# An element-wise causal attention kernel: one fold moved to another step, two sums joined, and the work at the start put in another order

## The chip, the cores and the metric

The kernel runs on one core of one Trainium2 chip. Its engines work side by side and meet only at semaphores: TensorE multiplies matrices (PE in the profile, PEld for its weight loads), VectorE (DVE) and GpSimd (POOL) do element-wise work and reductions, ScalarE (ACT) does exponentials, activations and copies out of the matrix accumulators, SyncE (SP) issues transfers. GpSimd issues transfers too, among them all that add into their target. The metric is the device time of one execution in microseconds (us). The kernel before takes 4008.09 us (median of three runs, 4007.45 to 4010.71).

## The reference

Input x has 8 batches of 512 tokens with 256 features. Four blocks follow each other, each added to x after a layer norm: attention A, a feed-forward net, attention B, and the same feed-forward net again.

```python
x = x + attn_a(layernorm(x), Wq, bq, Wk, bk, Wv, bv, Wo, bo)
x = x + ffn(layernorm(x), w1, w2, h1, h2, w3)
x = x + attn_b(layernorm(x), W_attn, b_attn, W_proj, b_proj)
x = x + ffn(layernorm(x), w1, w2, h1, h2, w3)
```

The change lies in attention A. It attends not between tokens but inside each token and head: with 16 heads of 64 channels,

```python
scores = einsum('bshq,bshk->bshqk', Q / 8, K)     # 64 x 64 for each token and head
scores = where(triu(ones((64, 64)), 1), -inf, scores)
w = softmax(scores, axis=-1)
attn = einsum('bshqk,bshk->bshq', w, V)
```

A score is the product of two single numbers, so no matrix engine can help: for every token and head there are 2080 products, exponentials and weighted values. They are done element by element, with the tokens on the 128 partitions.

## The kernel before

**Groups.** Attention A takes the work in groups of 128 tokens by 4 heads (256 columns). There are 8 batches, 4 column groups g and 4 token tiles i, so 128 groups. For each group TensorE projects queries and values (`qv`) and keys (`pk`), ScalarE copies keys and queries to SBUF (`keep_qk`, L761, L762).

**Units.** The lower triangle of each 64 by 64 score matrix is cut into squares on the diagonal's steps: one square of side 32 for each head, two of 16, then 8, 4, 2, 1. A group has four units, and these are its four steps: unit 0 is the squares of 32 of two heads, unit 1 all squares of 16, unit 2 the squares of 32 of the other two heads, unit 3 all small ones. For each unit:

- `scores` multiplies queries and keys (L784), on GpSimd for units 0 and 2, in two instructions, and on VectorE for units 1 and 3;
- `exps` takes the exponential on ScalarE (L798);
- `weigh` multiplies by the values on VectorE (L808), so that a tile holds exponentials and weighted values side by side;
- units 0 to 2 are then **halved**: `halve` (L814) has GpSimd issue a transfer that adds the second half of the 4096-column tile onto the first, 1 MB;
- units 0 and 2 are halved once more by an addition on GpSimd, `fold` (L819);
- `gather` (L845) sums what is left along the rows, on VectorE, into a tile `red`;
- `add_rows` (L852) adds `red` into the group's accumulator `acc` on GpSimd. `small_squares` (L835 and L852) does this for the squares of 2 and 1;
- at the end `invert` (L856) and `divide` (L860) make the quotient, and TensorE transposes and projects it out.

**Steps.** `AttentionA.step(n)` writes out one step by hand. All engines but SyncE keep the order in which these lines run. There are 512 units, and a step has work of several of them: the scores of unit n, the exponentials of n-1, the weighing and halving of n-2, folds and gathers of n-3 and n-4, the division of n-5. A step has three parts, each ended by a `yield`. In what follows the steps of a group are named by n mod 4, which is the unit whose scores are computed.

| step | part | GpSimd, before | VectorE, before |
|---|---|---|---|
| 0 | A | scores of unit 0, first half; halving of unit 2; second half | weighing of unit 2; reciprocal |
| 0 | B | division; **fold of unit 0** | |
| 1 | A | | weighing of unit 3; gather of unit 1 |
| 1 | B | sum of unit 1; small squares; fold of unit 2 | scores of unit 1 |
| 1 | C | | **gather of unit 0** |
| 2 | A | scores of unit 2, first half; halving of unit 0; second half | weighing of unit 0 |
| 2 | B | **sum of unit 0** | |
| 2 | C | | gathers of unit 2 and of the squares of 8 and 4 |
| 3 | A | halving of unit 1 | weighing of unit 1 |
| 3 | B | sums of unit 2, of the squares of 8 and of 4 | scores of unit 3 |

The unit numbers belong to the group that the unit is of: in steps 0 and 1 the weighing, folding and gathering is of the group that began four steps before. A list `self.sums` holds sums until part B of the next step, or of the same one where the gather stood in part A.

**Between the parts** the main loop (at the end of `fast_path`) puts other work. `done` is a generator of the feed-forward nets and attention B of batches whose attention A is complete. It starts at step 75, and from there on is advanced in proportion to the steps, so that it fills the gaps of attention A. Before that, two things happen once. `fit_qkv(g)` subtracts a row from the projection weights of column group g (on GpSimd, but for g = 0 on VectorE), has SyncE load a bias row into them and store them to a scratch tensor in DRAM, out of which `load_w` loads them later. `prep = later_weights()` is a generator that prepares the later weights and bounds the scores: small work on braw (L421 to L432), products for w3 (L451), subtractions (L456) on GpSimd, loads and stores on SyncE, squares on ScalarE (L373, L374), 96 matrix products with one column (L382). It has 30 pieces.

`measure(b)` computes the layer norm's scales of batch b on VectorE and GpSimd.

Of the kernel before, what the change touches and what calls it, by code (L numbers as in the profile page):

```python
# [9 lines left out]
F32 = mybir.dt.float32  # L10
# [3 lines left out]
ALU = mybir.AluOpType  # L14
AX = mybir.AxisListType

P = 128
# [9 lines left out]
GW = GH * C  # L27
NG = HID // GW
# [256 lines left out]
def fast_path(ctx: ExitStack, tc: tile.TileContext, k, t, flag):  # L285

    nc = tc.nc
# [8 lines left out]
    ap_ = ctx.enter_context(tc.tile_pool(name="ap", bufs=2))  # L296
# [42 lines left out]
    def fit_qkv(g):  # L339

        wqv, wk = fitted[g]
        eng = nc.vector if g == 0 else nc.gpsimd
        qv_last = last_qv[:, g * 2 * GW : (g + 1) * 2 * GW].unsqueeze(1).to_broadcast([P, DC, 2 * GW])
        eng.tensor_tensor(wqv, wqv, qv_last, ALU.subtract)
        k_last = last_k[:, g * GW : (g + 1) * GW].unsqueeze(1).to_broadcast([P, DC, GW])
        eng.tensor_tensor(wk, wk, k_last, ALU.subtract)
        nc.sync.dma_start(wqv[P - 1 : P, DC - 1, :], t.b_qv[g : g + 1, :])
        nc.sync.dma_start(wk[P - 1 : P, DC - 1, :], t.b_a[1:2, g * GW : (g + 1) * GW])
        nc.sync.dma_start(wqv_d[g].rearrange("p (c f) -> p c f", c=DC), wqv)
        nc.sync.dma_start(wk_d[g].rearrange("p (c f) -> p c f", c=DC), wk)  # L350
# [253 lines left out]
    class AttentionA:  # L604
# [33 lines left out]
        def step(self, n):  # L638
# [13 lines left out]
            b, i, g, u = self.at(n + 40)  # L652
            if u == 0 and g == 0 and i == 0 and b > 0:
                self.x[b] = load_x(b)
            b, i, g, u = self.at(n + 10)
            if u == 0 and g == 0 and i == 0:
                self.measure(b)
            b, i, g, u = self.at(n + 8)
            if u == 0 and g == 0:
                self.live["xn"] = normed(self.x[b][:, i, :], *self.rn[b, i], "a")  # L660
            b, i, g, u = self.at(n - 5)
            if u == NU - 1:
                self.invert(b, i, g)
            b, i, g, u = self.at(n - 4)
            if u == 1:
                self.gather(b, i, g, u)
            b, i, g, u = self.at(n + 7)
# [11 lines left out]
            b, i, g, u = self.at(n - 5)  # L679
# [3 lines left out]
            if u == NU - 1:  # L683
                self.small_squares(b, i, g)

            b, i, g, u = self.at(n - 4)
            if u == 0:
                self.fold(b, i, g, u)
            b, i, g, u = self.at(n - 3)
            if u == 2:  # L690
                self.fold(b, i, g, u)
# [14 lines left out]
                self.project(b, i, g)  # L706
            yield
            b, i, g, u = self.at(n - 4)
            if u == 2:
                self.gather(b, i, g, u)  # L710
            b, i, g, u = self.at(n - 5)
            if u == 0:
                self.gather(b, i, g, u)
            b, i, g, u = self.at(n - 3)
            if u == NU - 1:
                self.gather(b, i, g, u)
            b, i, g, u = self.at(n - 7)
            if u == NU - 1:
                nc.scalar.copy(self.live["att"], self.live.pop("pta"))
# [118 lines left out]
        def gather(self, b, i, g, n_u):  # L838


            w = self.live.pop((b, i, g, n_u))
            for n, off, nsq, cols in squares(units[n_u]):
                if n > 2:
                    red = ap_.tile([P, 2, nsq * n], F32, tag=f"red{nsq * n}", name=f"red_{b}_{i}_{g}_{n_u}_{n}", bufs=2 + (n < 32))
                    nc.vector.tensor_reduce(red, self.columns_of(w, n, off, nsq), AX.X, ALU.add)  # L845
                    self.sums.append((b, i, g, n, cols, red))

        def add_rows(self, b, i, g, n, cols, part):

# [491 lines left out]
    with tc.manual_schedule(engines={ET.PE, ET.DVE, ET.Activation, ET.Pool}):  # L1341
        a = AttentionA()
        prep = later_weights()
        fit_qkv(0)
        weights = None
        done, spent = after_a(), 0
        for n in range(-10, a.steps):
            for part, _ in enumerate(a.step(n)):
                if n >= 2:
                    next(prep, None)  # L1350
                while 3 * spent * each < total * (3 * (n - each - 11) + part + 1):
                    spent += next(done)
            if 0 <= n < NG - 1:
                fit_qkv(n + 1)
        for _ in done:
            pass
    judge()
# [86 lines left out]
```

## Time and profile before

| what | value |
|---|---|
| median of three runs | 4008.09 us |
| the profiled execution, its own time | 4009.55 us |
| its span in the profile | 4007.6 us |
| VectorE busy | 3376.7 us (84%) |
| GpSimd busy | 3098.1 us (77%) |
| TensorE busy | 2958.0 us (74%) |
| ScalarE busy | 2337.2 us (58%) |
| transfers of GpSimd's queue, share of the 16 DMA engines' span | 62.9% |
| additions of `red` into `acc` on GpSimd, 128x256, 384 of them | 759 ns each |
| the same, 128x128, 256 of them | 701 ns each |
| folds (L819), 256 of them | 2512 ns each |

The profile is one execution as the hardware profiler recorded it. Busy time is the time in which an engine had an instruction at work, its share is of the span. The profile also lists groups of instructions with the mean time of one and the idle time of the engine just before them, the waits by engine with what ended them, and the instructions in order of time. A line number is that of the kernel's text, and a tile has its program name with the buffer number left out. Records of GpSimd overlap a little, so the distance from one start to the next is the better measure of what an instruction takes there.

### The profile page before, as it was taken

The page shows a single profiled execution, that of the slowest core. Times are in us where ns is not written, and L with a number is a line of the kernel's source. Part 1 is how long each engine was busy: PE and PEld are TensorE (multiplying, and loading weights), DVE is VectorE, ACT ScalarE, POOL GpSimd, SP SyncE. Part 2 cuts the span into 40 slices and gives each one's busy share as a digit, 9 for nine tenths or more (in the row PEclk, how much of TensorE's full clock was granted, in tenths as well). Part 3 has the DMA queues.
Part 4 walks back from the last instruction along what each step waited for, and adds up shares of the span by engine and source line. Part 5 has one row for each costly group of instructions (what it writes and reads, how often), then busy time and mean ns, then how long its engine had stood idle before and what let it go on. Part 6 is the DMA issues. An engine that isn't in the chain of part 4 may idle for free.

```text
span 4007.6 us, 37678 instructions
## 1 busy us (share of the span) xinstructions
PE 2958.0 (74%) x12328; PEld 2012.2 (50%) x12328; DVE 3376.7 (84%) x3777; ACT 2337.2 (58%) x3145; POOL 3098.1 (77%) x3051
## 2 busy tenths in 40 slices
PE   1543478777876888768787788768787778768988
PEld 0311145355653656346553566346653556436847
DVE  4899988998889888998989988998889988897115
ACT  2433465666755766666755767567656667555342
POOL 6688888887888887887888888888888878886211
PEclk7555689888987989889897889879898899879999
DMA  8566777668776777668776688668877687767304
GB/s 240 114 141 145 146 182 182 147 161 199 199 162 126 195 188 196 150 147 210 174 192 139 168 198 214 147 131 198 195 181 151 154 199 205 155 133 210 126 29 167
DMA packets 118653, 671.07 MB, mean 167 GB/s; under 512 B 12704, under 2 KB 31915, under 8 KB 43824
## 3 DMA queue, kind: packets, MB, share of 16 engines
q0 software_dynamic: 78336, 570.46, 62.9%
q1 hardware_dynamic: 40112, 98.11, 6.8%
q8 instruction: 100, 1.64, 0.2%
q14 instruction: 105, 0.86, 0.1%
HBM read 255.90 MB, written 9.96 MB: 66 GB/s over the span
## 4 chain that ended last, share of the span: by engine, by line
DVE 38%; PE 16%; POOL 14%; DMA 12%; issue 8%; ACT 8%; POOLq 0%; DVEq 0%; ACTq 0%
DVE red L845 15%; DMA w<-w 12%; DVE w L808 10%; PE ph L1120 5%; ACT w L798 3%; POOL w L819 3%; DVE ws L808 3%; POOL w L784 3%; PE pqkb L1167 3%; DVE ws L784 3%; POOL acc L852 3%; DVE w L784 2%; POOL w L814 2%; DVE acc L856 2%; POOL h L1036 2%
## 5 line engine op out<-in xcount | busy, mean ns | idle before, releaser
L798 ACT ACTIVATE w<-w 128x2048 f32<-128x2048 f32 x384 | 734.2, 1913 | 653.8 <-POOL w L784 440.8
L1120 PE MATMUL ph<-h,hidden 128*128 128x512 f32 x4096 | 1047.9, 412 | 77.4 <-POOL h L1036 45.5
L784 POOL TENSOR_TENSOR w<-k 128x1024 f32<-128x1024 f32 x512 | 1076.2, 2102 | 9.6 <-ACT k L762 9.0
L1120 PEld LDWEIGHTS ph<-h,hidden 128*128 128x128 f32 x4096 | 795.3, 196 | 282.1 <-POOL h L1036 55.9
L808 DVE TENSOR_TENSOR w<-w,qv 128x1024 f32<-128x1024 f32 x768 | 899.8, 1213 | 22.4 <-ACT w L798 22.3
L845 DVE TENSOR_REDUCE red<-w 128x128 f32<-128x1024 f32 (+1 forms) x384 | 601.8, 1567 | 171.6 <-DMA w<-w 94.6
L819 POOL TENSOR_TENSOR w<-w 128x1024 f32<-128x1024 f32 x256 | 643.1, 2512 | 72.5 <-DMA w<-w 71.9
L814 POOL DMA_DIRECT2D w<-w x384 | 337.1, 878 | 339.7 <-issue 134.8
L852 POOL TENSOR_TENSOR acc<-acc,red 128x256 f32<-128x256 f32 (+1 forms) x640 | 471.0, 736 | 152.3 <-DVE red L845 124.5
L845 DVE TENSOR_REDUCE red<-ws 128x256 f32<-128x2048 f32 (+1 forms) x256 | 435.5, 1743 | 0.0
L746 PE MATMUL qv<-wqv,xnta 128*128 128x512 f32 x512 | 299.3, 715 | 89.9 <-DVE ws L808 82.4
L808 DVE TENSOR_TENSOR ws<-ws,qv 128x1024 f32<-128x1024 f32 (+3 forms) x512 | 294.7, 638 | 49.4 <-ACT ws L798 49.4
L1052 PE MATMUL pw<-xnt,gate 128*128 128x512 f32 (+2 forms) x1152 | 298.8, 419 | 24.9 <-ACT silu L1028 18.0
L784 DVE TENSOR_TENSOR w<-qv,k 128x1024 f32<-128x1024 f32 x256 | 301.3, 1219 | 3.6
L784 DVE TENSOR_TENSOR ws<-qv,k 128x1024 f32<-128x1024 f32 (+3 forms) x512 | 299.8, 648 | 0.0
L868 PE MATMUL bank<-ident,acc 128*128 128x128 f32 x256 | 64.3, 341 | 287.5 <-ACT k L761 287.1
L798 ACT ACTIVATE ws<-ws 128x1920 f32<-128x1920 f32 x128 | 231.5, 1809 | 75.3 <-DVE ws L784 74.7
L1052 PEld LDWEIGHTS pw<-xnt,gate 128*128 128x128 f32 x1152 | 227.6, 213 | 82.1 <-ACT silu L1028 22.3
L1229 ACT ACTIVATE eb<-psb 128x256 f32<-128x256 f32 (+3 forms) x512 | 182.2, 443 | 146.6 <-PE psb L1226 146.3
L1146 PE MATMUL pof<-w,h 128*128 128x256 f32 x1024 | 247.9, 396 | 19.4 <-ACT h L1085 19.4
L1085 ACT ACTIVATE h<-ph,s_sb 128x512 fp32r<-128x512 f32 (+1 forms) x256 | 171.1, 688 | 145.9 <-PE ph L1120 144.6
L856 DVE RECIPROCAL acc<-acc 128x256 f32<-128x256 f32 x128 | 223.2, 1744 | 12.3 <-POOL acc L852 12.3
(143 smaller groups left out, 4723.5 us busy)
## 6 DMA issues: line engine op xcount, KB each, us to landing
w<-w POOLq DMA_DIRECT2D x384, 1024.0 KB, 7.7
hidden<-in_h POOLq DMA_DIRECT2D x128, 1024.0 KB, 7.9
gate<-in_w12p POOLq DMA_DIRECT2D x32, 1024.0 KB, 9.0
w<-w_d SPq DMA_DIRECT2D x16, 1024.0 KB, 12.0
wqv<-wqv_d SPq DMA_DIRECT2D x31, 512.0 KB
wo<-in_wo SPq DMA_DIRECT2D x32, 256.0 KB, 7.4
wbqk<-wbqk_d SPq DMA_DIRECT2D x8, 1024.0 KB
w<-in_h SPq DMA_DIRECT2D x8, 1024.0 KB, 7.0
```

The source lines that it names most:

```text
L746: nc.tensor.matmul(qv.rearrange("p j f -> p (j f)"), xnt[:, c, :], wqv[:, c, :], start=(c == 0), stop=(c == DC - 1),)
L784: eng.tensor_tensor(e, rows(q).to_broadcast(shape), columns(kt[:, 0]).to_broadcast(shape), ALU.mult)
L798: nc.scalar.activation(e, e, AF.Exp, scale=C**-0.5)
L808: nc.vector.tensor_tensor(ev, e, columns(qv[:, 1]).to_broadcast(list(e.shape)), ALU.mult)
L814: nc.gpsimd.dma_start(w[:, :2048], w[:, 2048:], accum_op=ALU.add)
L819: nc.gpsimd.tensor_tensor(w[:, :1024], w[:, :1024], w[:, 1024:2048], ALU.add)
L845: nc.vector.tensor_reduce(red, self.columns_of(w, n, off, nsq), AX.X, ALU.add)
L852: nc.gpsimd.tensor_tensor(rows, rows, part.rearrange("p a (x i) -> p a x i", i=n), ALU.add)
L856: nc.vector.reciprocal(acc[:, 0, :], acc[:, 0, :])
L1052: nc.tensor.matmul(pj[:, toks], w[:, m % 4, j, c, :], xs[:, p, c, toks], start=(p == 0 and c == 0), stop=(p == 1 and c == DC - 1),)
L1120: nc.tensor.matmul(pss[j], w[:, j, c, :], h_in(p, c), start=(p == 0 and c == 0), stop=(p == 1 and c == MC - 1),)
L1146: nc.tensor.matmul(po, h(0, c)[:, i * P : (i + 1) * P], w3[:, c, :], start=(c == 0), stop=False)
```

## The change

Four things are changed.

1. The fold of unit 0 moves from part B of step 0 to part C of the step 3 before it, two parts earlier. The gather of unit 0 moves from part C of step 1 to part C of step 0.
2. The gathers of units 0 and 2 write the two halves of one tile `red`, and one `add_rows` over all 256 columns adds both. The sum of unit 0 in step 2 goes away. The tile of the squares of 32 has one buffer, where it had two.
3. `measure(0)` runs before `fit_qkv(0)`.
4. `fit_qkv(1)`, `(2)`, `(3)` run after steps 4, 14 and 24, where they ran after steps 0, 1 and 2. `prep` is advanced once a step, in part C from step 3 on, where it was advanced in each of the three parts from step 2 on.

```diff
             if u == 0 and g == 0 and i == 0:
-                self.measure(b)
+                if b > 0:
+                    self.measure(b)
...
-            b, i, g, u = self.at(n - 4)
-            if u == 0:
-                self.fold(b, i, g, u)
             b, i, g, u = self.at(n - 3)
             if u == 2:
                 self.fold(b, i, g, u)
...
             b, i, g, u = self.at(n - 4)
-            if u == 2:
-                self.gather(b, i, g, u)
-            b, i, g, u = self.at(n - 5)
-            if u == 0:
+            if u in (0, 2):
                 self.gather(b, i, g, u)
             b, i, g, u = self.at(n - 3)
             if u == NU - 1:
                 self.gather(b, i, g, u)
+            if u == 0:
+                self.fold(b, i, g, u)
...
                 if n > 2:
-                    red = ap_.tile([P, 2, nsq * n], F32, tag=f"red{nsq * n}", name=f"red_{b}_{i}_{g}_{n_u}_{n}", bufs=2 + (n < 32))
-                    nc.vector.tensor_reduce(red, self.columns_of(w, n, off, nsq), AX.X, ALU.add)
-                    self.sums.append((b, i, g, n, cols, red))
+                    if n_u != 2:
+                        self.live["red", n] = ap_.tile(
+                            [P, 2, GW // 2], F32, tag=f"red{n // 32}", name=f"red{n}_{b}_{i}_{g}", bufs=1 if n == 32 else 3
+                        )
+                    red = self.live["red", n]
+                    part = red[:, :, cols.start // 2 : cols.stop // 2]
+                    nc.vector.tensor_reduce(part, self.columns_of(w, n, off, nsq), AX.X, ALU.add)
+                    if n_u != 0:
+                        self.sums.append((b, i, g, n, slice(0, GW), red))
...
         a = AttentionA()
         prep = later_weights()
+        a.measure(0)
         fit_qkv(0)
...
             for part, _ in enumerate(a.step(n)):
-                if n >= 2:
+                if n >= 3 and part == 2:
                     next(prep, None)
...
-            if 0 <= n < NG - 1:
-                fit_qkv(n + 1)
+            if n in (4, 14, 24):
+                fit_qkv(n // 10 + 1)
```

## The prediction

> **What bounds the kernel now.** I read the page first, then a table of busy time by stretch, then who waits in the long middle stretch, then the instructions of one undisturbed group.
>
> ```profile
> span 4007.6 us, 37678 instructions
> PE 2958.0 (74%) x12328; PEld 2012.2 (50%) x12328; DVE 3376.7 (84%) x3777; ACT 2337.2 (58%) x3145; POOL 3098.1 (77%) x3051
> ```
>
> VectorE is busiest, GpSimd close behind. By stretch (busy time of PE, PEld, DVE, ACT, POOL, then clock, share of the DMA engines, rate):
>
> ```profile
> 0.00:60.00 60.00, 15.01 (x32) 7.18 (x32) 22.55 (x33) 19.64 (x27) 34.13 (x39) 0.83 0.71 214
> 60.00:130.00 70.00, 20.52 (x94) 18.00 (x95) 39.14 (x37) 16.77 (x15) 43.17 (x38) 0.53 0.69 193
> 130.00:200.00 70.00, 32.01 (x67) 15.76 (x66) 65.81 (x75) 29.93 (x30) 56.69 (x50) 0.60 0.63 130
> 300.00:500.00 200.00, 78.22 (x138) 37.55 (x139) 199.59 (x211) 80.54 (x84) 173.10 (x156) 0.56 0.70 146
> 1500.00:2000.00 500.00, 389.68 (x1651) 268.74 (x1650) 449.02 (x503) 324.75 (x430) 417.01 (x407) 0.88 0.74 175
> ```
>
> Three regimes. In the first 200 us VectorE idles 37.5 + 30.9 + 4.2 = 72.6 us. Up to 500 us, with attention A alone, it is full: 23.7 us a group. From then to 3500 us it is 90% busy, some 27 us a group. What it waits for there (500 to 3500 us; total, times, longest):
>
> ```profile
> DVE red L845 <- DMA w<-w: 84.0, 37, 4.9
> DVE red L845 <- POOL w L819: 73.3, 28, 5.6
> DVE silu L1031 <- ACT silu L1028: 47.4, 23, 5.0
> ```
>
> The first is the gather of unit 1 waiting for its halving, the second mostly the gather of unit 2 waiting for its fold. One undisturbed group (start, duration; x2 or x3 are merged):
>
> ```profile
> 350.66 0.87 POOL L814 DMA_DIRECT2D w<-w  x1 [2.69 <-issue]
> 351.27 2.35 POOL L852 TENSOR_TENSOR acc<-acc,red 128x128 f32<-128x128 f32 x3
> 353.57 1.96 POOL L784 TENSOR_TENSOR w<-k 128x1024 f32<-128x1024 f32 x1
> 355.47 0.85 POOL L814 DMA_DIRECT2D w<-w  x1
> 358.00 1.00 POOL L860 TENSOR_TENSOR acc<-acc 128x256 f32<-128x256 f32 x1
> 358.68 2.63 POOL L819 TENSOR_TENSOR w<-w 128x1024 f32<-128x1024 f32 x1
> 364.25 2.36 POOL L819 TENSOR_TENSOR w<-w 128x1024 f32<-128x1024 f32 x1
> 367.06 1.21 DVE L845 TENSOR_REDUCE red<-w 128x128 f32<-128x1024 f32 x1
> ```
>
> 350.66 is the halving of unit 1 and 355.47 that of unit 2; the first fold is unit 0's, the second unit 2's, which VectorE gathers at 367.06 without a wait. GpSimd's one idle gap, 2.69 us, is its slack of a group.
>
> **What the Trainium skill says.** DMA: Bandwidth & Descriptors, Rules for kernel authors: issue a transfer early and wait late. Unit 0's fold does this now: halving to fold took 15 us in the groups I followed, against 6.9 us at least and 7.9 us in the median to landing from 500 to 3500 us. GPSIMD Engine Reference, Elementwise: an addition of two SBUF operands of 2048 columns takes 4497 ns. A fold of 1024 takes 2.36 to 2.63 us here, in agreement.
>
> **The change part by part.**
>
> *Sums joined.* Each group loses two additions of 128x128 at 701 ns and gains one of 128x256 at 759 ns: 643 ns less, 128 times, 82 us of GpSimd. None of it lies on VectorE, whose gathers stay the same in number and size. It widens GpSimd's slack from 2.7 to 3.3 us; that is the cover, so I cost it at 0 (-20 at best, where GpSimd is late in crowded groups; 0 at worst). The single buffer costs nothing: the next gather of unit 0 waits for GpSimd's sum, and the fold that it waits for anyway stands behind this sum.
>
> *Gather of unit 0 earlier.* 1.21 us of VectorE move ahead of the gather of unit 1, which gives that halving 1.2 us more. 37 waits of 84.0/37 = 2.3 us lose at most 40 us if each of them gives up to 1.2. Part comes back at unit 2's gather, before which VectorE's work is unchanged: I take -20 (0 to -40). Unit 0's own wait for its fold, 2.6 us in all, may go.
>
> *Fold of unit 0 earlier.* It now stands between the three sums and the next scores: 2.35 us later for the first half of the scores, for unit 2's halving behind it, and for every later transfer of that queue up to the old place of the fold. Is its own halving there? It was issued 5.9 us before unit 1's, whose issue and sums take 2.9: 8.8 us against 6.9 to 8.2 (nine in ten). Group by group it would wait 10.6 us in all, nearly all in one group. Late scores of unit 0 delay ScalarE by 1.6 us a group, but VectorE weighs them 2.2 us after the exponential's new end (362.6 against 364.8 in the group above); +5 (0 to 20) for the feed-forward work behind ScalarE.
>
> Unit 2 is the open point. Its halving moves from 355.47 to 357.82, lands at best 6.95 us later, 364.77, and its fold, which began at 364.25, is 0.5 us late. It ended 0.45 us before the gather. So VectorE loses about 0.1 us in such a group, 0.4 with a landing of 7.3. The loop is short: issue 0.6, sums 2.3, fold 2.35, scores 1.9, transfer 7.0, fold 2.35, then VectorE's gathers and weighing of unit 1, 7.3 from 367.06 to the next halving: 23.8 us against VectorE's 23.7. I worked the same shift through every group from its issue, landing, fold and gather times. If a landing is later only where 6.95 us from the new issue demands it, unit 2's waits go from 74 to 88 us: +14. If each landing is later by the whole shift, to 180: +106. I take +14, because where waits are long now, landings take 10 to 16 us behind other transfers, and a later issue then only shortens the queue. The 13 groups before step 75 add 3 (10).
>
> *The start.* Halvings of unit 0 begin at 41.0, 78.7, 124.5, 154.8 and 178.7 us in the first five groups, then every 23.7. The excess is four gaps, 137.7 - 94.8 = 43 us, from work on GpSimd (fits of 3.7 us each right after the first scores, 7.2 us of waiting for a crowded transfer) and 24.7 us in one wait: ScalarE stood 21.9 us for a load of sk. After the change, in order: `measure(0)` first brings the keys forward by 2 to 3 us, until the bias row (issued 17.11) holds them. From keys at 25: scores 3.9, exponential 1.9, weighing 2.4, first halving at 33.4. Its fold waits for the landing at 40.4, then fold, scores, the braw piece and fit, the sums, fold and scores: second group at about 59.7 (78.7 now). Then 23.7 a group plus what of the prepared pieces exceeds the slack of 3.3: about 3 (w3, 1.4 a step), 3, 6 (fit 3.7 with two L456 of 2.35), 0 and 3.7 (the last fit): seventh group at 194 where it is 226. That is 32 us; 7 off for crowded transfers, whose landings took up to 16 us at the start: -25 (-5 to -40). The moved SyncE work: fit 1's stores stand ahead of the column load of step 9, fit 3's ahead of the second load of step 25, needed at step 29, four steps or 24 us on; w3's store holds the queue until step 12, and behind it are loads needed at step 15. sk is asked for after step 16 and squared at step 19. All hidden; if one is not, ScalarE stands again, up to 20 us.
>
> Sum: -25 + 14 + 3 - 20 - 2.6 + 5 = -26 us, on its own 4009.55 as on the median, which is 1.5 less: **3982 us**.
>
> **Rivals.** *Unit 2's transfer becomes the bound.* Place: the gather of unit 2, behind fold and halving. Price as above, +106 + 10, against -25 - 40 - 2.6: 4056 us. It decides the sign once unit 2 loses over 0.26 us more a group than I count, on average (the 26 us and the 8 us of the measurement, over 128). For it: 0.45 us of room, and a loop as long as VectorE's own. Against it: the queue argument. *No change to see.* The start's gain is eaten, since 28 us of prepared work move from idle time into a full phase with 3.3 us of slack a group; likewise if the bounding of scores still makes ScalarE stand: about 4004 us. *Better.* The even load also takes a third of the fold waits (25 us) and all of the 40 at unit 1: 3982 - 45 = 3937 us. *The fold isn't where the text puts it*: excluded, in the built order it stands right behind the three sums.
>
> **How the numbers follow.** My forecast 0.55, its own range 3962 to 3999; unit 2 as bound 0.17; no change 0.14; better 0.14. A measurement can tell 0.2% from nothing, 8 us: faster 0.54 + 0.14 + 0.01 = 0.69, same 0.14, slower 0.17. The range leaves out about the lower half of "better" and the upper half of "unit 2 as bound": 3940 to 4040.
>
> **What would show it.** VectorE's idle time in the first 200 us down from 72.6 to about 45, and the seventh group some 25 to 30 us earlier. GpSimd's additions 128 fewer, its busy time down by about 82 us. Between 500 and 3500 us: waits of the gather for the transfer well under 84 us, waits for the fold near 88, not 150. In the undisturbed groups a period of 23.7 to 24.0 us, and a new GpSimd wait for the transfer just ahead of unit 2's fold. The forecast is wrong if that period is 24.3 or more, or if ScalarE again stands at L374.

## The result, and the profile after

The changed kernel takes 4039.92 us (median of four runs, 4038.21 to 4043.97), against 4008.87 us for the kernel before in the same measurement: a ratio of 1.0079, with a 95% interval of 1.0061 to 1.0096. It is 0.8% slower. I forecast 3982 us. The profiled execution took 4038.21 us, with a span of 4036.4 us; before it was 4007.6 us, so +28.8 us are to be found.

In the kernel after, the lines have moved: the halving is L811, the fold L816, the gather L847, `add_rows` L855, the scores L781, the exponential L795, the weighing L805, the division L863. The page of the profile after, with the costs of the fold, the sums of `red` and the gathers (busy time, mean ns of one, idle time ahead of them and what ended it):

```profile
span 4036.4 us, 37531 instructions
...
PE 2977.2 (74%) x12328; PEld 2020.8 (50%) x12328; DVE 3386.3 (84%) x3777; ACT 2340.0 (58%) x3145; POOL 3075.7 (76%) x2923
...
L847 DVE TENSOR_REDUCE red<-w 128x128 f32<-128x1024 f32 (+1 forms) x384 | 600.0, 1563 | 201.0 <-POOL w L816 168.2
L816 POOL TENSOR_TENSOR w<-w 128x1024 f32<-128x1024 f32 x256 | 607.8, 2374 | 108.1 <-DMA w<-w 105.7
...
L855 POOL TENSOR_TENSOR acc<-acc,red 128x256 f32<-128x256 f32 x512 | 410.6, 802 | 189.3 <-DVE red L847 153.6
```

GpSimd does 128 additions fewer, as the change says. VectorE, the busiest engine, stands 168.2 us at gathers whose fold is not done; before it was 76.9 us. The busy time by stretch (PE, PEld, DVE, ACT, POOL, then clock, share of the DMA engines, rate):

```profile
0.00:60.00 60.00, 21.97 (x36) 9.55 (x36) 31.72 (x40) 21.08 (x28) 32.49 (x38) 0.79 0.70 201
60.00:130.00 70.00, 20.07 (x34) 8.81 (x34) 59.63 (x61) 23.39 (x23) 62.29 (x54) 0.50 0.73 179
130.00:200.00 70.00, 35.62 (x98) 23.55 (x98) 59.53 (x60) 27.44 (x25) 55.72 (x47) 0.50 0.82 199
300.00:500.00 200.00, 78.97 (x139) 37.24 (x137) 195.61 (x205) 77.81 (x82) 169.84 (x145) 0.53 0.67 140
1500.00:2000.00 500.00, 388.45 (x1652) 268.39 (x1650) 447.75 (x503) 325.23 (x427) 409.67 (x388) 0.89 0.74 176
```

The start is better: VectorE idles 28.28 + 10.37 + 10.47 = 49.1 us of the first 200, where it was 72.6. From 300 to 500 us, where it had been idle for 0.4 us, it now idles for 4.4. What it waits for from 500 to 3500 us (total, times, longest):

```profile
DVE red L847 <- POOL w L816: 133.3, 80, 8.7
DVE silu L1034 <- ACT silu L1031: 58.4, 32, 5.0
DVE xnt L986 <- ACT xnt L979: 37.0, 20, 3.4
DVE red L847 <- DMA w<-w: 27.8, 19, 2.9
DVE h L1094 <- ACT ph L1090: 25.2, 29, 2.4
```

The wait of unit 1's gather for its transfer fell from 84.0 to 27.8 us, more than I had hoped. The wait for a fold rose from 73.3 to 133.3 us, in 80 places instead of 28.

I took the issue of unit 0's halving of each group as a mark and asked where the 28.8 us came in. The seventh group is reached 20.5 us earlier (205.6 where it was 226.1). Eleven groups later 11.0 us of this are gone. From the 18th group to the last the loss is 32.8 us, and 5.6 us come after it: -20.5 + 11.0 + 32.8 + 5.6 = 28.9. Among the 110 groups from the 18th on, the 25 with a period under 24.6 us before, which nothing disturbs, lose 16.9 us, 0.68 each; the 50 with a period of 29 us and more lose 13.9, and the 35 between lose 2.0.

So the new cost can be seen in its purest form in an undisturbed group. It takes 24.4 us now, where it took 23.7. GpSimd's instructions of one (start, duration, idle time before it):

```profile
417.61 1.96 POOL L781 TENSOR_TENSOR w<-k 128x1024 f32<-128x1024 f32 x1
419.50 0.86 POOL L811 DMA_DIRECT2D w<-w  x1
420.11 2.24 POOL L781 TENSOR_TENSOR w<-k 128x1024 f32<-128x1024 f32 x1
422.03 1.00 POOL L863 TENSOR_TENSOR acc<-acc 128x256 f32<-128x256 f32 x1
423.77 0.73 POOL L855 TENSOR_TENSOR acc<-acc,red 128x256 f32<-128x256 f32 x1 [0.75 <-DVE red L847]
424.46 0.62 POOL L832 TENSOR_TENSOR ws<-ws 128x256 f32<-128x256 f32 x1
425.16 1.66 POOL L855 TENSOR_TENSOR acc<-acc,ws 128x256 f32<-128x256 f32 x2
426.77 2.36 POOL L816 TENSOR_TENSOR w<-w 128x1024 f32<-128x1024 f32 x1
```

And VectorE's in the same microseconds:

```profile
421.34 2.29 DVE L847 TENSOR_REDUCE red<-w 128x256 f32<-128x2048 f32 x1
423.67 2.36 DVE L781 TENSOR_TENSOR w<-qv,k 128x1024 f32<-128x1024 f32 x2
425.94 0.41 DVE L802 TENSOR_TENSOR acc<-acc,qv 128x256 f32<-128x256 f32 x1
426.26 2.35 DVE L805 TENSOR_TENSOR w<-w,qv 128x1024 f32<-128x1024 f32 x2
429.17 1.22 DVE L847 TENSOR_REDUCE red<-w 128x128 f32<-128x1024 f32 x1 [0.56 <-POOL w L816]
```

VectorE gathers unit 1 (421.34). GpSimd stood 0.75 us for just this, then makes its sum, the small squares and the fold of unit 2 one behind the other, until 429.13: 5.5 us after the gather's end. VectorE's work up to the gather of unit 2 is over after 5.0 us, and it stands 0.56 us. The fold did not wait for its transfer. The same stretch of VectorE before the change:

```profile
358.75 2.28 DVE L845 TENSOR_REDUCE red<-w 128x256 f32<-128x2048 f32 x1
361.07 2.36 DVE L784 TENSOR_TENSOR w<-qv,k 128x1024 f32<-128x1024 f32 x2
363.34 1.21 DVE L845 TENSOR_REDUCE red<-w 128x128 f32<-128x1024 f32 x1
364.47 0.41 DVE L805 TENSOR_TENSOR acc<-acc,qv 128x256 f32<-128x256 f32 x1
364.80 2.35 DVE L808 TENSOR_TENSOR w<-w,qv 128x1024 f32<-128x1024 f32 x2
```

At 363.34 stands the gather of unit 0. It took 1.13 us from start to start between the gather of unit 1 and that of unit 2 (367.06), and this was the time in which GpSimd finished. The change moved it ahead of unit 1's gather. The fold had ended 0.45 us before it was wanted; 0.45 - 1.13 = -0.68 us, which is the mean loss of 0.68 us in the 25 undisturbed groups.

### The profile page after: what moved, and what is told of

The parts are those of the page before. It is cut to its first block, busy times and chain, and to the rows that moved or that the text cites. A ratio compares the mean times of both kernels' runs of the same rounds, so it can differ in the third digit from the quotient of the medians.

```text
span 4036.4 us, 37531 instructions
## 1 busy us (share of the span) xinstructions
PE 2977.2 (74%) x12328; PEld 2020.8 (50%) x12328; DVE 3386.3 (84%) x3777; ACT 2340.0 (58%) x3145; POOL 3075.7 (76%) x2923
## 4 chain that ended last, share of the span: by engine, by line
DVE 34%; POOL 19%; PE 19%; issue 8%; ACT 7%; DMA 6%; POOLq 0%; ACTq 0%; DVEq 0%
DVE red L847 14%; DVE w L805 7%; PE ph L1123 6%; DMA w<-w 6%; POOL w L816 5%; POOL acc L855 5%; DVE ws L805 4%; POOL w L781 3%; ACT w L795 3%; DVE ws L781 2%; PE pqkb L1170 2%; DVE acc L859 2%; POOL h L1039 2%; PE pyb L1237 2%; POOL w L811 1%
## 5 line engine op out<-in xcount | busy, mean ns | idle before, releaser
L795 ACT ACTIVATE w<-w 128x2048 f32<-128x2048 f32 x384 | 733.8, 1913 | 730.3 <-POOL w L781 609.0
L781 POOL TENSOR_TENSOR w<-k 128x1024 f32<-128x1024 f32 x512 | 1074.4, 2099 | 17.1 <-ACT k L759 16.8
L805 DVE TENSOR_TENSOR w<-w,qv 128x1024 f32<-128x1024 f32 x768 | 900.1, 1214 | 22.7 <-ACT w L795 22.7
L847 DVE TENSOR_REDUCE red<-w 128x128 f32<-128x1024 f32 (+1 forms) x384 | 600.0, 1563 | 201.0 <-POOL w L816 168.2
L816 POOL TENSOR_TENSOR w<-w 128x1024 f32<-128x1024 f32 x256 | 607.8, 2374 | 108.1 <-DMA w<-w 105.7
L811 POOL DMA_DIRECT2D w<-w x384 | 336.1, 875 | 317.5 <-ACT w L795 108.2
L855 POOL TENSOR_TENSOR acc<-acc,red 128x256 f32<-128x256 f32 x512 | 410.6, 802 | 189.3 <-DVE red L847 153.6
L847 DVE TENSOR_REDUCE red<-ws 128x256 f32<-128x2048 f32 (+1 forms) x256 | 435.5, 1743 | 0.0
L781 DVE TENSOR_TENSOR w<-qv,k 128x1024 f32<-128x1024 f32 x256 | 301.4, 1219 | 3.6
L805 DVE TENSOR_TENSOR ws<-ws,qv 128x1024 f32<-128x1024 f32 (+3 forms) x512 | 299.3, 649 | 5.1 <-ACT ws L795 4.8
L781 DVE TENSOR_TENSOR ws<-qv,k 128x1024 f32<-128x1024 f32 (+3 forms) x512 | 299.9, 650 | 0.0
L795 ACT ACTIVATE ws<-ws 128x1920 f32<-128x1920 f32 x128 | 231.7, 1810 | 64.6 <-DVE ws L781 63.9
L743 PEld LDWEIGHTS qv<-wqv,xnta 128*128 128x128 f32 x512 | 107.6, 225 | 296.7 <-issue 209.3
```

The costliest lines, as they stand in the source:

```text
L743: nc.tensor.matmul(qv.rearrange("p j f -> p (j f)"), xnt[:, c, :], wqv[:, c, :], start=(c == 0), stop=(c == DC - 1),)
L781: eng.tensor_tensor(e, rows(q).to_broadcast(shape), columns(kt[:, 0]).to_broadcast(shape), ALU.mult)
L795: nc.scalar.activation(e, e, AF.Exp, scale=C**-0.5)
L805: nc.vector.tensor_tensor(ev, e, columns(qv[:, 1]).to_broadcast(list(e.shape)), ALU.mult)
L811: nc.gpsimd.dma_start(w[:, :2048], w[:, 2048:], accum_op=ALU.add)
L816: nc.gpsimd.tensor_tensor(w[:, :1024], w[:, :1024], w[:, 1024:2048], ALU.add)
```

## The experiments

All ratios are against the kernel before on the same chip; the bracket is the 95% interval. Experiments 1 to 4, 5 to 8, and 9 to 12 were measured together. The kernel before took 4010.57, 4011.83 and 4011.79 us in these three sets, so that times of different sets can be set beside each other to a microsecond or two.

**1 and 2: the two halves of the change.** `start_only` is the kernel before with points 3 and 4 of the change (measure first, weight fits after steps 4, 14 and 24, one prepared piece a step). `groups_only` is the changed kernel with these undone.

```diff
 # start_only, against the kernel before
...
+        a.measure(0)
         fit_qkv(0)
...
-                if n >= 2:
+                if n >= 3 and part == 2:
                     next(prep, None)
...
-            if 0 <= n < NG - 1:
-                fit_qkv(n + 1)
+            if n in (4, 14, 24):
+                fit_qkv(n // 10 + 1)
```

> The kernel before with the new order at the beginning alone (measure(0) first, fits after steps 4, 14 and 24, one prepared piece a step); fold, gathers and sums as before. The trace of the changed kernel has the seventh group's halving of unit 0 at 205.6 us where it was at 226.1, and loses 4 us in the group after it, where the bounding of the scores lies. Both theories: the start's gain is real and independent of the groups, the period of the undisturbed groups stays at 23.7 us, and the time is 4009 - 16 = 3993 us (3985 to 4000). If it is 4005 or more, the gain of the start in the changed kernel is no property of the start.

> The changed kernel with the old order at the beginning: the moved fold and gather and the joined sums alone. Both theories: the loss lies in the groups, undisturbed groups at 24.4 us, and the time is 4040 + 16 = 4056 us (4048 to 4064).

Measured: `start_only` 3996.38 us, ratio 0.9964 [0.9950, 0.9979], a gain of 14 us. Its undisturbed groups take 23.7 us. `groups_only` 4057.53 us, 1.0111 [1.0095, 1.0128], a loss of 47 us; its undisturbed groups take 24.4 us, and from 500 to 3500 us VectorE waits 128.9 us for folds and 34.8 us for transfers, as in the changed kernel. So the whole loss is in the group's new order, and the start is a gain, if a smaller one than forecast.

**3 and 4: which of the moves.** `gather_back` is the changed kernel with the gather of unit 0 back in step 1. `both_back` has the fold back too, and so keeps only the joined sums and the new start.

```diff
 # gather_back, against the changed kernel
             b, i, g, u = self.at(n - 4)
-            if u in (0, 2):
+            if u == 2:
+                self.gather(b, i, g, u)
+            b, i, g, u = self.at(n - 5)
+            if u == 0:
                 self.gather(b, i, g, u)
 # both_back: this, and in part B ahead of the fold of unit 2
+            b, i, g, u = self.at(n - 4)
+            if u == 0:
+                self.fold(b, i, g, u)
 # and in part C
-            if u == 0:
-                self.fold(b, i, g, u)
```

> The changed kernel with the gather of unit 0 back in part C of step 1, behind the gather of unit 1; the fold of unit 0 stays early, the sums stay joined. Theory 1 (cover): the gather of unit 0 used to stand between the gathers of units 1 and 2 and covered GpSimd's sum of unit 1, its small squares and the fold of unit 2; with it back, the undisturbed period falls from 24.4 to between 23.7 and 24.1 us and VectorE's waits for the fold in 500 to 3500 us fall from 133 us to under 100, its waits for the transfer at unit 1 rise from 28 back to 60 or more; time 4015 to 4030. Theory 2 (late transfer): the fold of unit 0 ahead of unit 2's halving is the cause, so nothing changes where it was: period 24.4, time 4036 to 4044.

> The changed kernel with the fold and the gather of unit 0 both back in their old places; the sums stay joined and the start is new. Both theories: period 23.7 us, time as with the new start alone less what GpSimd's 643 ns a group are worth: 3993 us less 0 to 10, 3983 to 3995. If it is over 4000, the joined sums cost something by themselves (a third theory: the single buffer of red makes the next gather of unit 0 wait).

Measured: `gather_back` 4026.89 us, 1.0038 [1.0023, 1.0052]; `both_back` 3978.98 us, 0.9920 [0.9903, 0.9936], which beats both kernels. The early fold with the gather left in place therefore costs 48 us (3978.98 to 4026.89), and the gather's move another 13 (to 4039.92). The undisturbed groups take 24.1 us at best in `gather_back` and 23.7 in `both_back`. In the first of these the reason is another than in the changed kernel. GpSimd in `gather_back`:

```profile
340.36 0.84 POOL L814 DMA_DIRECT2D w<-w  x1
...
347.33 2.36 POOL L819 TENSOR_TENSOR w<-w 128x1024 f32<-128x1024 f32 x1 [0.48 <-DMA w<-w]
...
364.44 0.85 POOL L814 DMA_DIRECT2D w<-w  x1
```

Unit 2's fold stands for its transfer, which takes 6.97 us from issue to fold. The loop from one halving of unit 2 to the next, 24.08 us, is closed: transfer 6.97, fold until VectorE's gather 2.39, VectorE's work until the weighing of unit 1 is done 6.79, then 0.54 until the halving of unit 1 is issued, its issue 0.61, the three sums 2.57, the fold of unit 0 2.31, the first scores 1.90. The early fold made this loop longer than VectorE's own 23.7 us. The landing is a part of it, and where it takes longer the group does too: the 25 undisturbed groups from the 18th on lose 16.3 us against `both_back`, 0.65 each. A nearer suspect is not to blame: that the early fold of unit 0 stands for its own halving costs GpSimd 7.0 us in the whole run. With the gather moved as well, the fold of unit 2 is late for the reason shown above, and the transfer has 0.35 us to spare (419.50 + 6.92 = 426.42, the median landing of this unit in the first groups, against the fold at 426.77). The waits from 500 to 3500 us, first `gather_back`:

```profile
DVE red L850 <- POOL w L819: 98.3, 38, 6.9
DVE red L850 <- DMA w<-w: 51.6, 26, 4.7
...
DVE h L1097 <- ACT ph L1093: 39.2, 38, 5.4
```

and `both_back`:

```profile
DVE red L851 <- POOL w L820: 77.2, 31, 6.0
DVE red L851 <- DMA w<-w: 65.0, 32, 5.5
```

With the early fold VectorE thus waits 21 us more for folds and 13 us less for transfers. The third line of `gather_back`, VectorE's subtraction in the feed-forward net that waits for ScalarE's `ph`, stands at 12.6 us in `both_back` and has grown by 27.

**5 and 6: is it the transfer's start or GpSimd's path?** `halve_first` issues unit 2's halving ahead of both halves of the next scores, so that the transfer starts 1.9 us earlier, and leaves the rest of the changed kernel alone. `halve_first_gather_back` does this in `gather_back`.

```diff
+            if weighed[3] == 2:
+                self.halve(*weighed)
             if on_pool:
                 half = self.scores(*unit)
                 next(half)
-            if weighed[0] is not None:
+            if weighed[3] in (0, 1):
                 self.halve(*weighed)
```

> The changed kernel with unit 2's halving issued ahead of both halves of the scores of unit 0, behind the early fold; that is 1.9 us earlier, nearly its old place in time. Fold and gather of unit 0 stay early. Theory 1 (cover): with the gather of unit 0 ahead of unit 1's, GpSimd's sum of unit 1, small squares and fold still set unit 2's gather; the undisturbed period stays at 24.3 to 24.4 us, time 4020 to 4040. Theory 2 (late transfer): the transfer is no longer late, period 23.7 to 23.8, time 3975 to 4000, with waits for the fold in 500 to 3500 us under 90 us.

> As the run before, and the gather of unit 0 back behind the gather of unit 1. With both suspected causes taken away and the fold still early, both theories together say: undisturbed period 23.7 us, and a time as with fold and gather both back, 3979 us (3970 to 3990). If the period stays at 24.1 as with the gather alone put back, neither the transfer nor the cover is what the early fold costs, and its place ahead of the scores itself is (scores and exponential of unit 0 later).

Measured: `halve_first` 4049.97 us, 1.0092 [1.0075, 1.0109]. That is above the 4020 to 4040 us expected, and no better than the changed kernel. Its undisturbed groups still take 24.4 us: in one of them the transfer lands at 322.14 us, 2.2 us before the fold begins at 324.38, and VectorE stands 0.56 us at the gather of unit 2, as in the changed kernel. With the transfer in good time, the path behind unit 1's gather holds them alone. `halve_first_gather_back` 4017.62 us, 1.0011 [1.0004, 1.0018], where 3979 was expected. Its undisturbed groups do take 23.7 us, so that with the transfer early and the gather back both causes are gone there. These two kernels differ in the place of unit 0's gather alone: it costs 0.7 us in an undisturbed group and 32 us in all. But the 50 crowded groups lose 24.4 us against the kernel before, where `both_back` gains 7.8 in them. What the early fold costs in the crowded groups is thus not the late transfer alone.

**7 and 8: shorten the path by putting the fold first.** `fold2_first` has GpSimd fold unit 2 ahead of the sum of unit 1 and of the small squares. `both_back_fold2_first` does the same in `both_back`.

```diff
+            b, i, g, u = self.at(n - 3)
+            if u == 2:
+                self.fold(b, i, g, u)
             for args in self.sums:
                 self.add_rows(*args)
...
-            b, i, g, u = self.at(n - 3)
-            if u == 2:
-                self.fold(b, i, g, u)
```

> The changed kernel with the fold of unit 2 ahead of the sum of unit 1 and the small squares on GpSimd, so that it waits for its transfer alone and no longer for VectorE's gather of unit 1. Theory 1: the path over the sum is cut, and what is left is the transfer's loop, as with the gather put back: undisturbed period 24.1 us, time 4020 to 4032. Theory 2 alone: the transfer set the pace already, period 24.4, time 4036 to 4044.

> New start and joined sums, fold and gather of unit 0 in their old places (3979 us), and the fold of unit 2 ahead of the sum of unit 1 and the small squares. In crowded groups VectorE waits 77 us for the fold: if GpSimd is late there because of what stands ahead of the fold, these fall to about 40 us and the time to 3950 to 3970; if the transfer is late, GpSimd stands at the fold instead of doing the sums, and the time is 3979 to 3995.

Measured: 4233.09 us, 1.0546 [1.0529, 1.0564], and 4123.94 us, 1.0280 [1.0263, 1.0298]; both far off. GpSimd of `fold2_first`, and its largest wait from 500 to 3500 us:

```profile
412.72 0.83 POOL L811 DMA_DIRECT2D w<-w  x1
...
419.89 2.36 POOL L816 TENSOR_TENSOR w<-w 128x1024 f32<-128x1024 f32 x1 [3.67 <-DMA w<-w]
422.21 0.72 POOL L855 TENSOR_TENSOR acc<-acc,red 128x256 f32<-128x256 f32 x1
```

```profile
POOL w L816 <- DMA w<-w: 553.0, 150, 12.8
```

The fold now stands at the head of GpSimd's queue until the transfer has landed, and the 3 us of sums that used to fill this time stand behind it. Over the whole run GpSimd is idle for 632 us ahead of unit 2's folds. Ahead of all folds it had been 108.1 us in the changed kernel, and 72.5 before. The Trainium skill says that GpSimd's execution queue is strict first in, first out (Perfetto Trace Analysis, Per-engine timelines, Tensor Engine Instruction); this trace agrees: unit 1's gather ended at 416.56, and its sum, free to run, began at 422.21, behind the fold. I had reckoned with the price of the path and not with that of the queue.

**9: what does the fold's place cost GpSimd's other work?** `fold_mid` is `both_back` with the fold of unit 0 between the halving of unit 2 and the second half of the scores: unit 2's halving is as early as before the change, and the scores of unit 0 are later by one fold.

```diff
             if weighed[0] is not None:
                 self.halve(*weighed)
+            b, i, g, u = self.at(n - 4)
+            if u == 0:
+                self.fold(b, i, g, u)
             if on_pool:
                 next(half, None)
```

> New start, joined sums, gather of unit 0 in its old place; the fold of unit 0 stands between unit 2's halving and the second half of the scores of unit 0 (old place: behind the scores and the division). The halving keeps its old time, the second half of the scores and with it ScalarE's exponential come 2.4 us later, as with the early fold. With fold and gather back the time is 3979 us, with the fold early and the gather back 4027 us. If the late transfer is what the early fold costs: period 23.7 us and 3975 to 3990. If the late scores are (ScalarE behind, and with it the feed-forward net in crowded groups): period 23.7 us, but 4000 to 4025, with the waits of L1094's subtraction for ScalarE near 39 us instead of 13.

Measured: 3995.31 us, 0.9958 [0.9943, 0.9972], 16 us over `both_back`. Undisturbed groups take 23.7 us. ScalarE's exponential waits 447.7 us for GpSimd's scores from 500 to 3500 us, where it is 314.7 in `both_back`, 300.6 before and 396.4 after. One of VectorE's waits that follows from it, in `fold_mid`:

```profile
DVE h L1098 <- ACT ph L1094: 35.4, 34, 5.4
```

In `both_back` this wait is 12.6 us. The time lies between the two ranges expected (3975 to 3990, 4000 to 4025); the wait is near the 39 us that stood for the late scores. So 16 of the 48 us of the early fold are there with the second half of the scores late and the halving in time. That the other 32 go with the later halving is not shown: in `halve_first_gather_back` unit 2's halving is later than in the old order by some 0.4 us alone (the fold's 2.31 less the scores' 1.90), and 39 of the 48 us are there (3978.98 to 4017.62).

**10 and 11: give the cover back without moving the gather.** In `small_first` VectorE gathers the squares of 8 and 4 ahead of unit 2, not behind it. Nothing else in the changed kernel is touched. The 3.3 us of these gathers then stand between unit 1's and unit 2's. `both_back_small_first` does it in `both_back`.

```diff
 # small_first, against the changed kernel
+            b, i, g, u = self.at(n - 3)
+            if u == NU - 1:
+                self.gather(b, i, g, u)
             b, i, g, u = self.at(n - 4)
             if u in (0, 2):
                 self.gather(b, i, g, u)
             b, i, g, u = self.at(n - 3)
-            if u == NU - 1:
-                self.gather(b, i, g, u)
             if u == 0:
                 self.fold(b, i, g, u)
```

> The changed kernel with the gathers of the small squares (3.4 us of VectorE) ahead of the gather of unit 2 in step 2. This gives GpSimd's sum, small squares and fold, and unit 2's transfer, 3.4 us more cover and moves nothing on GpSimd. Theories 1 and 2 alike: undisturbed period 23.7 us, waits for the fold in 500 to 3500 us from 133 to under 70 us, time 3965 to 4000. If the early fold costs by the late scores instead, the period is 23.7 but the time stays over 4005.

> New start and joined sums with fold and gather of unit 0 in their old places (3979 us), and the gathers of the small squares ahead of that of unit 2. Waits for the fold are 77 us there: with 3.4 us more cover, they fall to 30 or so, time 3940 to 3965. If the crowded groups are bound by GpSimd or by the transfers as a whole, the wait only moves to another place, and the time stays at 3970 to 3985.

Measured: `small_first` 4007.32 us, 0.9990 [0.9983, 0.9997], 33 us less than the changed kernel, and its undisturbed groups take 23.7 us again. VectorE in one of them:

```profile
345.44 2.35 DVE L806 TENSOR_TENSOR w<-w,qv 128x1024 f32<-128x1024 f32 x2
347.71 3.40 DVE L848 TENSOR_REDUCE red<-ws 128x256 f32<-128x2048 f32 x2
351.03 1.21 DVE L848 TENSOR_REDUCE red<-w 128x128 f32<-128x1024 f32 x1
```

The fold of unit 2 ended at 348.32 in this group, when VectorE was at the gathers of the small squares (347.71); unit 2's gather at 351.03 does not wait. From 500 to 3500 us the waits for a fold fall from 133.3 to 76.5 us. Both miss what was expected (under 70 us of these waits, 3965 to 4000 us), and the time is over the 4005 named as the mark of late scores. The early fold, whose price `gather_back` shows, is still in this kernel. In addition GpSimd now stands 38.8 us at unit 0's folds for their own halvings, where it was 4.5 in the changed kernel. `both_back_small_first` takes 3966.85 us, 0.9884 [0.9865, 0.9902], the fastest of all the kernels here. Its waits from 500 to 3500 us:

```profile
DVE red L851 <- DMA w<-w: 79.4, 36, 5.3
...
DVE ws L809 <- ACT ws L799: 44.0, 28, 2.4
DVE w L809 <- ACT w L799: 31.9, 26, 3.6
...
DVE red L851 <- POOL w L820: 20.1, 13, 2.9
```

Of 77.2 us at folds 57 are gone, but the run is only 12 us shorter, just above the 3940 to 3965 us expected: the wait for the transfer of unit 1 has grown by 14 us (65.0 to 79.4) and the two for ScalarE's exponentials by 37 (26.3 to 44.0 and 12.9 to 31.9). A shorter wait hands its time to the next late result.

**12: the joined sums by themselves.** `joined_only` is the kernel before with point 2 of the change.

```diff
-                    red = ap_.tile([P, 2, nsq * n], F32, tag=f"red{nsq * n}", name=f"red_{b}_{i}_{g}_{n_u}_{n}", bufs=2 + (n < 32))
-                    nc.vector.tensor_reduce(red, self.columns_of(w, n, off, nsq), AX.X, ALU.add)
-                    self.sums.append((b, i, g, n, cols, red))
+                    if n_u != 2:
+                        self.live["red", n] = ap_.tile(
+                            [P, 2, GW // 2], F32, tag=f"red{n // 32}", name=f"red{n}_{b}_{i}_{g}", bufs=1 if n == 32 else 3
+                        )
+                    red = self.live["red", n]
+                    part = red[:, :, cols.start // 2 : cols.stop // 2]
+                    nc.vector.tensor_reduce(part, self.columns_of(w, n, off, nsq), AX.X, ALU.add)
+                    if n_u != 0:
+                        self.sums.append((b, i, g, n, slice(0, GW), red))
```

> The kernel before with the joined sums alone. From the new start alone (3996 us) to the new start with joined sums (3979 us) it was 17 us: if that is the joined sums' own worth, this kernel is at 4010 - 17 = 3993 us (3985 to 4000). If it is within 5 us of before, the gain needed the new start.

Measured: 3994.86 us, 0.9953 [0.9936, 0.9970], a gain of 17 us. The undisturbed groups are unchanged at 23.7 us; the crowded 50 gain 9.6 and the 35 between 7.9 us. VectorE's wait for unit 1's transfer falls from 84.0 to 63.7 us, the wait for folds stays at 73.3.

## Why the prediction was wrong, point by point

The sum as forecast and as the runs give it:

| part | forecast, us | measured, us | from |
|---|---|---|---|
| the start | -25 | -14 | `start_only` |
| sums joined | 0 | -17 | `joined_only` |
| fold of unit 0 earlier (unit 2's transfer, first groups, ScalarE) | +14 + 3 + 5 | +48 | `gather_back` less `both_back` |
| gather of unit 0 earlier, with its own fold wait | -20 - 2.6 | +13 | changed kernel less `gather_back` |
| sum | -26 | +30 | +31 by the medians |

The gather's line missed by 36 us and the fold's by 26; the start and the sums together were better than forecast by 6. The two large lines depend on the order in which the moves are undone. The 13 us are what the gather's move adds where unit 2's transfer is late already; with that transfer early (`halve_first` less `halve_first_gather_back`) the same move costs 32 us. The gather moved while the fold keeps its old place was not run.

**The step that failed in kind: the gather of unit 0.** "Part comes back at unit 2's gather, before which VectorE's work is unchanged." The amount of VectorE's work is unchanged, but its place is not. The gather left the stretch between the gathers of units 1 and 2, and GpSimd's sum, small squares and fold run in exactly this stretch, since they begin when unit 1 has been gathered. I had both numbers in hand, the 0.45 us by which the fold was early and the 1.21 us of the gather, and put the 0.45 against the transfer alone. The half of the step that I did see was right: from `gather_back` to the changed kernel, which differ in the gather's place alone, the waits for unit 1's transfer went down by 24 us (51.6 to 27.8), where the forecast had 20. But the waits at the folds went up by 35 us (98.3 to 133.3), where it had nothing. That the cover is the cause in undisturbed groups is shown by `halve_first`, which leaves the period at 24.4 with the transfer early, while the gather put back beside it brings 23.7. `small_first`, which puts other work in the gap, takes 33 us off and brings 23.7 too; it gives the transfer more time as well, so that alone it would not tell the two apart.

**Unit 2's transfer: the mechanism was right, the size was not.** The loop that I wrote down is the one that sets the pace in `gather_back`. I made it 23.8 us with 2.3 for three sums; the joined sums take 2.57, and it is 24.08. That is 0.3 us over what I reckoned where the landing is at its shortest, and more where it is not: against `both_back` the 25 undisturbed groups lose 0.65 us in the mean. The sign-deciding bound was 0.26 us a group on average, and the sums' growth alone reached it there. In the crowded groups I took the low end (+14, "a later issue then only shortens the queue"). The queue argument has something for it: the median landing of unit 2's halving from 500 to 3500 us is 7.6 us in `gather_back` and 8.4 in `both_back`, and the wait for folds, which the +14 priced, is 21 us longer. But `gather_back` lies 18.6 us over `both_back` in the 50 crowded groups and 8.5 in the 35 between, beside 16.3 in the 25 undisturbed ones, and the wait for folds alone does not make that up. The rival that made this transfer the bound forecast 4056 us and the right sign; in the changed kernel, though, its mark is missing: unit 2's fold starts behind GpSimd's own work in the undisturbed groups, not behind a transfer.

**ScalarE.** +5 (0 to 20) for late scores; in `fold_mid`, where the second half of the scores and the division are late, it is 16 us. The range held it and the value taken was too low. In `gather_back` VectorE's wait for ScalarE's `ph` grew by 27 us, more than its wait for folds. "VectorE weighs them 2.2 us after the exponential's new end" is true of the undisturbed groups, which `fold_mid` leaves at 23.7; the cost is in the groups with feed-forward work behind ScalarE.

**The joined sums.** Costed at 0, with -20 at best "where GpSimd is late in crowded groups". It was nearly the best. The wait that shrank is that of unit 1's gather for its transfer, by 20 us.

**The start.** Up to the seventh group mechanism and size were right: VectorE's idle time in the first 200 us fell from 72.6 to 49.1 us (forecast 45), the first halving came at 33.3 us (33.4) and the second at 60.7 (59.7), and ScalarE no longer stands at L374. The text had the seventh group at 194 us, and 7 us later for crowded transfers. In `start_only`, where nothing else is changed, it came at 201.1 us, 25.0 earlier than before. In the changed kernel it came at 205.6 us, so some 4 to 5 us belong to the longer groups. The crowding is largest in the fourth group, GpSimd after the change:

```profile
135.22 0.85 POOL L811 DMA_DIRECT2D w<-w  x1
...
149.94 2.34 POOL L816 TENSOR_TENSOR w<-w 128x1024 f32<-128x1024 f32 x1 [6.81 <-DMA w<-w]
```

and SyncE, a little earlier:

```profile
132.68 7.10 SPq L368 DMA_DIRECT2D sqv<-in_wqv  x2
```

Unit 2's fold began 14.7 us after its halving was issued. Two loads of 1 MB for the bounding of the scores, asked for from 132.68 us on, run beside the halving, with a third at 140.53; the DMA engines are busy for 99% of the time from 135 to 150 us. VectorE stood 7.4 us at the gather. From 121.07 to 126.91 us GpSimd was busy with a prepared subtraction and the two parts of a fit, ahead of the halving of unit 1.

What the sum left out comes behind the seventh group. The bounding of the scores ends in seven small instructions on VectorE (L389 to L402). Before, they ran from 129.96 to 138.90 us, in a stretch where VectorE had idle time. Now they stand where it is full; in `start_only`:

```profile
236.87 0.48 DVE L399 TENSOR_REDUCE best<-ptop 1x3 f32<-1x384 f32 x1
...
237.68 3.94 DVE L402 TENSOR_SCALAR over<-over 1x2 f32<-1x2 f32 x1
241.54 2.33 DVE L809 TENSOR_TENSOR ws<-ws,qv 128x1024 f32<-128x1024 f32 x4
```

The four from L399 to L402 take 4.67 us from start to start and the three before them 0.66, and the eighth group takes 29.0 us where an undisturbed one takes 23.7. That is the kind of loss that "no change" described, if smaller. L402 works on two numbers and is recorded with 0.16 us in the kernel before (138.74); why it is 3.94 here is not explained. From the 18th group on `start_only` is within 1 us of the kernel before. Its profiled run, the fastest of five, is 19.8 us shorter than that of the kernel before; no trace shows the 6 us that separate this from the gain of 14 us by the medians.

**The other rivals.** "Better" wanted the even load to take a third of the fold waits; they nearly doubled. "No change" was right that the start's gain would be eaten, but mostly by the groups; the pieces that moved took 5 us of it.

**The marks named beforehand.** A period of 24.3 us or more in the undisturbed groups was to refute the forecast, and it was 24.4. Waits for the transfer under 84 us: yes. Waits for folds near 88: no, 133.3. A new wait of GpSimd for unit 2's transfer: in `gather_back` yes, in the changed kernel not in such groups. GpSimd's busy time down by 82 us: no, by 22.4; a joined sum makes the three that follow each other 0.27 us longer, and the record of the removed one began 0.29 us before that of the scores ahead of it ended (371.00 against 369.08 + 2.21), so that 0.70 - 0.29 - 0.27 = 0.14 us of busy time goes per group, 18 us in all.

**What stays open.** The 32 us that `gather_back` loses beyond those of `fold_mid` are not split further. `halve_first_gather_back` shows that an earlier halving gives 9 us of them back over the whole run (4026.89 to 4017.62) and not more. Against `fold_mid` (3995.31 us) it has 15 us more of VectorE's waits for unit 1's transfer (64.7 and 49.5 us) and 4 more for folds, and I did not find which order of halving, fold and scores makes them. The two waits for ScalarE's silu and xnt rise by 11 and 9 us in the changed kernel, not in `gather_back`: they go with the gather's move, but I tried nothing on them. Nor did I follow the 5.6 us behind the last group's mark.

## What to carry to other kernels

An instruction on the busiest engine is not only a cost: where it stands between two gathers it is the time in which another engine finishes. Before moving it, measure for each pair of dependent points how long the other engine's path between them is and how much of the busiest engine's own work lies between them; an even load over the steps says nothing of this. When the cover is short, fill the gap with other work of the waiting engine (`small_first`), and do not put the awaited instruction at the head of an in-order queue that has other work to do (`fold2_first`).

## What the runs showed of the hardware that I had not expected

A fold of unit 0 is recorded with 2649 ns in the mean before the change and 2374 ns after it, with the same operands. In the old place it follows the division, whose 1.00 us record it overlaps by 0.32 us; from start to start it takes 2.50 us there and 2.32 us in its new place (402.40 to 404.72).

A sum's size counts for little on GpSimd. Three sums in a row of which one had 128 columns took 2.30 us from start to start of what follows, three of 256 columns take 2.57, so that doubling one costs 0.27 us. The sum that goes away for it had a record of 0.70 us.

A fold that waits at the head of GpSimd's queue holds up the ready work behind it: in `fold2_first` GpSimd stood 553 us at folds from 500 to 3500 us, and the run is 193 us longer than that of the changed kernel, with the same work in another order.
